# Layer 1: the 64-row update products of two neighbouring feature chunks made in one stretch

## The chip, the core and the metric

The kernel runs on one core of a Trainium2 chip. A core has TensorE (PE in the profile; its weight loads are PEld), VectorE (DVE), ScalarE (ACT), GpSimd (POOL) and SyncE (SP), which run side by side and wait for one another by semaphores. The metric is the device time of one execution, in microseconds; the figure given is the median of several executions. All arithmetic is in 32-bit floats.

## What is computed

A stack of four adaptive feed-forward layers is applied to 64 sequences of 32 tokens with 512 features, 2048 rows in all, each with a residual sum. The change lies in the second of them, called layer 1. Its first half is a gated feed-forward block in which each sequence has its own low-rank update (rank 16), chosen by an index:

```python
def lora_add(base, inp, A, B):
    Ab = A[layer_idx][lora_indices]
    Bb = B[layer_idx][lora_indices]
    t = jnp.einsum('bri,bni->bnr', Ab, inp)
    return base + jnp.einsum('bor,bnr->bno', Bb, t) * SCALE
gate = lora_add(jnp.einsum('bnh,fh->bnf', x, W_gate), x, A_gate, B_gate)
up = lora_add(jnp.einsum('bnh,fh->bnf', x, W_up), x, A_up, B_up)
act = jax.nn.silu(gate) * up
down = lora_add(jnp.einsum('bnf,hf->bnh', act, W_down), act, A_down, B_down)
```

The hidden width F is 1376. What follows (a routed mixture of low-rank experts on top of a dense product) is not touched by the change.

## The kernel before

Layer 1 takes the 2048 rows in eight groups of 256 rows, two tiles of 128 rows (t = 0 and 1). The 1376 hidden features are cut into eleven chunks f of 128 (the last, f = 10, has 96).

**Seven block products.** Gate and up of one chunk and one group are a 2 x 2 block product: the blocks of the left side are the two tiles by the two halves of the 512 input features, those of the right side are gate and up by the same halves. It is made with seven products in place of eight, `p1` to `p7` (methods of `Group`, from line 557), each of two matmuls of 128 x 128 by 128 columns, on sums of weight blocks and of activations that are made beforehand. They accumulate in three PSUM tiles, each a whole bank of 128 x 512: `acc_a`, `acc_b` and `acc_c`, each with two buffers, so that chunk f + 2 takes over the buffers of chunk f. Since later products add to the same columns, partial sums are copied out by ACT in between (`kept`, line 551): `p1` and `u2` out of `acc_a`, `p5` out of `acc_c`. The next product on those columns waits for that copy.

**The update products.** `seconds(f)` (line 586) adds the low-rank updates. The first factor, `low_x`, holds the 16 rank values of four sequences on 64 partitions, upper half for tile 0, lower half for tile 1. So each update product contracts over 64 rows only: four products for a chunk (gate and up, by tile), alternating between the upper and the lower 64 rows. Tile 0 adds to `acc_b` (gate) and `acc_c` (up), tile 1 to columns 0 to 127 (gate) and 128 to 255 (up) of `acc_a`. After them the chunk is put together: ACT copies the gate of tile 1 out of `acc_a` (line 597), DVE makes the other three blocks by adding kept partial sums (598, 599, 600), ACT takes a tanh (603), and DVE makes `actT` (604, 605), which the down projection reads later. `gate`, `up` and `sg` have one buffer each.

**The order.** TensorE's order is fixed: `on_pe` (line 76) chains every matmul to the one before. In `features(f)` it runs over two chunks: p1 of f, p7 of f - 1, p5 and p2 of f, p4 and `seconds` of f - 1, then p6 and p3 of f. So each chunk's update products stand between its p4 and the next chunk's p6. Between the chunks 0 to 4, pieces of the previous group's output are put in (`choose`, `turn`, `base`, `out`). In the first group the weight sums are made on the way (`sums_of`). The orders of the other engines are made from the program by a scheduler; waits between engines are set by it wherever two engines touch the same tile. Loads go by SP's queue (`load_by`, with an order written out), gathers of the update weights (`Bg1`, `Bu1`, `Bd1`) by POOL's.

Of the kernel before, what the change touches and what calls it, by code (L numbers as in the profile page):

```python
# [28 lines left out]
ALU = mybir.AluOpType  # L29
# [4 lines left out]
P = 128  # L34
# [7 lines left out]
FC = [(o, min(P, F1 - o)) for o in range(0, F1, P)]  # L42
# [358 lines left out]
def layer1(c, kp, x_in, x_out, sums):  # L401
# [5 lines left out]
    tc, nc, a = c.tc, c.nc, c.a  # L407
# [3 lines left out]
    NFC = len(FC)  # L411
# [5 lines left out]
    with ExitStack() as ctx:  # L417
# [31 lines left out]
        def product(out, lhsT, rhs, start, stop, more=False):  # L449
            c.on_pe(nc.tensor.matmul(out, lhsT, rhs, start=start, stop=stop, skip_group_check=more))  # L450

        class Group:
# [130 lines left out]
            def p4(self, f):  # L583
                self.block(f, 4, self.a[f])

            def seconds(self, f):

                o, w = FC[f]
                acc_a, acc_b, acc_c = (v.pop(f) for v in (self.a, self.b, self.c))
                for u in range(2):  # L590
                    for t in range(G):
                        q = slice(t * P // 2, (t + 1) * P // 2)
                        out = (acc_b, acc_c)[u][:w, :P] if t == 0 else acc_a[:w, u * P:(u + 1) * P]
                        product(out, self.B[("Bg1", "Bu1")[u]][q, o:o + w], self.low_x[q, u, :], False, True, more=True)
                part = self.part.pop(f)
                gate, up = self.gate, self.up
                nc.scalar.copy(gate[:w, 1], acc_a[:w, :P])
                nc.vector.tensor_tensor(gate[:w, 0], acc_b[:w, :P], part["p1"][:w], ALU.add)
                nc.vector.tensor_tensor(up[:w, 1], acc_a[:w, P:2 * P], up[:w, 1], ALU.add)
                nc.vector.tensor_tensor(up[:w, 0], acc_c[:w, :P], part["u2"][:w], ALU.add)  # L600
                sg = tp.tile([P, N], F32, name="sg", bufs=1)
                gate, up = (v.rearrange("p t n -> p (t n)") for v in (gate, up))
                nc.scalar.activation(sg[:w], gate[:w], AF.Tanh, scale=0.5)
                nc.vector.scalar_tensor_tensor(sg[:w], sg[:w], 1.0, gate[:w], ALU.add, ALU.mult)
                nc.vector.scalar_tensor_tensor(self.actT[:w, f, :], sg[:w], 0.5, up[:w], ALU.mult, ALU.mult)
# [92 lines left out]
        t = gup.tile([P, 3, K2, F1], F32, name="sums_gate_up")  # L698
        blocks = {1: b11, 2: b21, 3: b22, 4: b12, 5: t[:, 0], 6: t[:, 1], 7: t[:, 2]}

        def sums_of(f):

            if f >= NFC:
                return
            o, w = FC[f]
            v11, v21, v12, v22, t1, t2, t3 = (v[:, :, o:o + w] for v in
                                              (b11, b21, b12, b22, t[:, 0], t[:, 1], t[:, 2]))
            nc.vector.tensor_tensor(t1, v12, v11, ALU.subtract)
            nc.vector.tensor_tensor(t3, v22, v12, ALU.subtract)
            nc.vector.tensor_tensor(t2, v22, t1, ALU.subtract)  # L710
            nc.vector.tensor_tensor(v12, v21, t2, ALU.subtract)
# [8 lines left out]
        for g, new in enumerate(groups):  # L720
            old = groups[g - 1] if g else None
            then = groups[g + 1] if g + 1 < len(groups) else None
            parts = [f for _ in range(5) for f in next(to_sum)]

            def features(f):
                if f < NFC:
                    new.p1(f)
                if f:
                    new.p7(f - 1)
                if f < NFC:  # L730
                    new.p5(f)
                    new.p2(f)
                elif then:
                    then.x(0)
                if f:
                    new.p4(f - 1)
                    new.seconds(f - 1)
                if f < NFC:
                    new.p6(f)
                    new.p3(f)  # L740
                if g == 0:
                    sums_of(f + 2)
                if f < len(parts):
                    parts[f]()

            features(0)
            if old:
                old.choose(0)
            features(1)
            if old:  # L750
                old.choose(1)
                old.weigh(0)
            features(2)
            if old:
                old.weigh(1)
            new.load_firsts("down")
            if then:
                then.load_firsts("x")
            features(3)
            if old:  # L760
                old.turn(0)
                old.base(0)
                old.out(0)
            features(4)
            if old:
                old.turn(1)
                old.base(1)
                old.out(1)
            for f in range(AHEAD):
                new.next_down(f)  # L770
            if then:
                then.load_x()
            for f in range(5, NFC + 1):
                features(f)
            if then:
                then.load_seconds()
                then.x(1)
            new.down(range(NFC - 1), False)
            if then:
                then.x_sums()  # L780
                then.low()
            new.low_down()
            new.down((NFC - 1,), True)
# [1026 lines left out]
```

## Time and profile before

| | |
|---|---|
| three executions | 3531.25, 3531.26, 3536.69 us, median 3531.26 |
| the profiled execution's own time | 3529.51 us |
| its span, first to last instruction | 3527.7 us |
| granted TensorE clock, mean | 0.997 of full speed |
| layer 1 in it | about 380 to 1010 us |
| calls of `seconds` | 88, eight groups of eleven chunks |

The span is what the profiler saw on the core; the execution's own time has 1.8 us around it. Of the views, the timeline is used most here: every instruction with its start and length, groups of equal ones merged. A 32-bit matmul shows as two records of the same name, so a block product is four records. Starts of matmuls are measured; their ends are modelled, so that records of one engine overlap.

### The profile page before, as it was taken

What the parts mean: (1) busy time and instruction counts of PE and PEld (TensorE: products, weight loads), DVE (VectorE), ACT (ScalarE), POOL (GpSimd) and SP (SyncE); (2) the same over time, 40 slices, a digit from 0 to 9 for tenths busy, and PEclk for the clock granted to TensorE, in tenths of its full rate; (3) what the DMA queues carried; (4) which work ended last, traced back from release to release, by engine and by line L of the source; (5) the groups of instructions that cost most, each with busy time, mean ns of one, the idle gap of its engine ahead of it and who ended that gap; (6) DMA issues with size and microseconds to landing.
All of it is one profiled execution on the core that took longest, in us unless ns stands there. A gap on an engine that the chain in (4) does not pass through costs nothing.

```text
span 3527.7 us, 65667 instructions
## 1 busy us (share of the span) xinstructions
PE 3472.3 (98%) x20736; PEld 2638.2 (75%) x20736; DVE 2085.3 (59%) x5116; ACT 1537.4 (44%) x4001; POOL 1615.1 (46%) x1608
## 2 busy tenths in 40 slices
PE   8999999999999999999999999999999999999999
PEld 4444788888866778777787787877877778778755
DVE  4443533433447766766767667676676776766433
ACT  4111222222225555555555555555555555555411
POOL 0112433232336645646456455564564655645232
PEclk9999999999999999999999999999999999999999
DMA  6013554454456787878878878878878788787721
GB/s 218 24 29 129 158 162 152 151 165 145 152 186 198 251 259 245 254 248 253 257 250 259 257 247 257 257 247 263 251 253 263 249 266 257 253 256 239 238 87 59
DMA packets 630634, 735.99 MB, mean 209 GB/s; under 512 B 64274, under 2 KB 480018, under 8 KB 630290
## 3 DMA queue, kind: packets, MB, share of 16 engines
q1 hardware_dynamic: 577810, 558.74, 51.0%
q0 software_dynamic: 50176, 168.86, 13.7%
q8 instruction: 168, 2.75, 0.3%
q10 hardware_dynamic: 2304, 4.20, 0.3%
q14 instruction: 176, 1.44, 0.1%
HBM read 689.61 MB, written 41.94 MB: 207 GB/s over the span
## 4 chain that ended last, share of the span: by engine, by line
PE 90%; DVE 4%; DMA 3%; issue 1%; ACT 1%; POOL 0%; SPq 0%; DVEq 0%; ACTq 0%; POOLq 0%
PE po L913 14%; PE sc L1195 12%; PE py L913 11%; PE pq L913 9%; PE prT_ps L908 6%; PE pkv L913 5%; PE acc_a L450 5%; PE pz L450 5%; PE pd L225 4%; PE po L1575 3%; PE ph L225 3%; PE acc_c L450 3%; PE acc_b L450 2%; PE po L450 2%; PE qkT_ps L908 2%; PE py L212 2%
## 5 line engine op out<-in xcount | busy, mean ns | idle before, releaser
L939 POOL DMA_INDIRECT vt<-in_v_rows,v_rows x512 | 511.2, 998 | 305.4 <-PE po L913 186.8
L1202 ACT ACTIVATE pr<-pr,low 128x544 f32<-128x544 f32 x512 | 383.4, 749 | 545.9 <-DVE low L1200 543.9
L1195 PE MATMUL sc<-kt,qT 128*128 128x288 f32 (+1 forms) x2048 | 554.6, 393 | 9.7 <-DVE low L1200 5.7
L1195 PEld LDWEIGHTS sc<-kt,qT 128*128 128x128 f32 x2048 | 384.8, 190 | 224.3 <-issue 123.5
L913 PE MATMUL po<-prT,vt 128*128 128x128 f32 x4096 | 543.6, 276 | 3.3 <-ACT prT L1213 2.0
L913 PEld LDWEIGHTS po<-prT,vt 128*128 128x128 f32 x4096 | 522.2, 192 | 32.8 <-ACT prT L1213 13.1
L1200 DVE CUSTOM_DVE_ANT_0 pr<-sc,mask 128x544 f32<-128x544 f32 x512 | 368.2, 719 | 203.3 <-PE sc L1195 202.9
L987 POOL TENSOR_TENSOR projected<-projected,swapped 128x512 f32<-128x512 f32 x160 | 208.1, 1300 | 310.1 <-DVE projected L986 286.9
L1207 DVE TENSOR_SCALAR pr<-pr,low 128x512 f32<-128x512 f32 x512 | 317.2, 620 | 12.8
L1213 ACT COPY prT<-prT_ps 128x512 f32<-128x512 f32 x512 | 293.3, 573 | 57.7 <-PE prT_ps L908 50.6
L908 PE MATMUL prT_ps<-ident,pr 128*128 128x128 f32 x2048 | 311.3, 275 | 0.8 <-DVE pr L1207 0.7
L1204 DVE RECIPROCAL low<-low 128x1 f32<-128x1 f32 x512 | 81.9, 160 | 282.0 <-ACT pr L1202 281.8
L908 PEld LDWEIGHTS prT_ps<-ident,pr 128*128 128x128 f32 x2048 | 237.9, 142 | 8.8 <-issue 1.1
L913 PE MATMUL py<-wo,oT 128*128 128x256 f32 x1024 | 241.8, 379 | 0.0
L913 PE MATMUL pq<-wp,x_sums 128*128 128x512 f32 x512 | 240.5, 593 | 0.5 <-DVE projected L1073 0.5
L913 PEld LDWEIGHTS py<-wo,oT 128*128 128x128 f32 x1024 | 186.5, 190 | 21.1
L130 POOL TENSOR_TENSOR rs<-rs,minus_half 128x4 f32<-128x4 f32 x160 | 179.8, 1123 | 22.9 <-DVE low L1204 15.3
L913 PE MATMUL pq<-wp,xT 128*128 128x512 f32 x384 | 182.7, 599 | 5.0 <-DVE projected L1073 5.0
L913 PE MATMUL py<-wo,o_sum 128*128 128x256 f32 x768 | 181.1, 379 | 2.3 <-DVE o_sum L1131 2.1
L1205 ACT ACTIVATE own_pr<-pr,low 128x32 f32<-128x32 f32 x512 | 164.9, 322 | 41.8 <-DVE low L1204 38.9
L988 POOL TENSOR_TENSOR projected<-projected,rs 128x512 f32<-128x512 f32 x160 | 171.9, 1074 | 7.9
L946 ACT COPY own_vt<-v 32x128 f32<-32x128 f32 x512 | 150.8, 295 | 53.7 <-PE po L913 42.2
(277 smaller groups left out, 6109.2 us busy)
## 6 DMA issues: line engine op xcount, KB each, us to landing
kt<-in_kT SPq DMA_DIRECT2D x2048, 64.0 KB
wp<-in_sums SPq DMA_DIRECT2D x192, 512.0 KB
wo<-out_sums SPq DMA_DIRECT2D x128, 512.0 KB
wp<-in_WqT SPq DMA_DIRECT2D x96, 512.0 KB
wo<-in_WoT SPq DMA_DIRECT2D x96, 512.0 KB
down1T<-in_down1T SPq DMA_DIRECT2D x80, 256.0 KB
wp<-in_WkT SPq DMA_DIRECT2D x32, 512.0 KB
xt<-x SPq DMA_DIRECT2D x48, 256.0 KB
```

The costliest lines, as they stand in the source:

```text
L130: self.nc.gpsimd.tensor_tensor(t, t, self.minus_half[:, :n], ALU.pow)
L225: c.on_pe(nc.tensor.matmul(out, lhsT, rhs, start=first and i == 0, stop=last and i == len(pairs) - 1))
L450: c.on_pe(nc.tensor.matmul(out, lhsT, rhs, start=start, stop=stop, skip_group_check=more))
L908: c.on_pe(nc.tensor.transpose(pt[:, m, :], piece, c.ident))
L913: c.on_pe(nc.tensor.matmul(out, lhsT, rhs, start=first and i == 0, stop=last and i == len(pairs) - 1))
L939: nc.gpsimd.indirect_dma_start(out=vts[b % 2][:, n, :], out_offset=None, in_=a["v_rows"], in_offset=bass.IndirectOffsetOnAxis(ap=rows[h][: ...
L987: nc.gpsimd.tensor_tensor(src, src, tmp, ALU.add)
L1195: c.on_pe(nc.tensor.matmul(sc[:, lo + n * PSIZE:lo + m * PSIZE].rearrange("p (n k) -> p n k", k=PSIZE), q, kt[:, n:m, g, :], start=True, s ...
L1200: nc.vector.tensor_tensor_reduce(pr[:, :NK], sc[:, lo:lo + NK], masks[h, b], -SCALE, 3.0e38, ALU.add, ALU.min, low[:, 0:1])
L1202: nc.scalar.activation(pr[:, :NK], pr[:, :NK], AF.Exp, bias=low[:, 0:1], scale=-1.0, accum_out=low[:, 1:2])
L1207: nc.vector.tensor_scalar(pr[:, :L], pr[:, :L], low[:, 2:3], None, ALU.mult)
L1213: last_prT.append(nc.scalar.copy(prT, pt).ins)
```

## The change

`seconds(f)` is cut in two: the products stay in `seconds(f, early)`, and putting the chunk together becomes `finish(f)`. In `features(f)` with odd f, the products of f - 1 are followed at once by those of f, the chunk whose p6, p3, p7 and p4 are still to come; for even f no update products are made, and only `finish(f - 1)` follows p4. Chunk 10 has no partner and stays alone.

For an early chunk the gate product of tile 1 can't go to columns 0 to 127 of `acc_a`, since the partial sum `u2` is still to be taken from those. It goes to columns 256 to 383, ACT copies these out under the name `rest`, and in `finish` DVE adds `rest` where for other chunks ACT copies.

```diff
-            def seconds(self, f):
+            def seconds(self, f, early):
                 o, w = FC[f]
-                acc_a, acc_b, acc_c = (v.pop(f) for v in (self.a, self.b, self.c))
+                acc_a, acc_b, acc_c = (v[f] for v in (self.a, self.b, self.c))
+                at = (2 if early else 0, 1)
                 for u in range(2):
                     for t in range(G):
                         q = slice(t * P // 2, (t + 1) * P // 2)
-                        out = (acc_b, acc_c)[u][:w, :P] if t == 0 else acc_a[:w, u * P:(u + 1) * P]
+                        out = (acc_b, acc_c)[u][:w, :P] if t == 0 else acc_a[:w, at[u] * P:(at[u] + 1) * P]
                         product(out, self.B[("Bg1", "Bu1")[u]][q, o:o + w], self.low_x[q, u, :], False, True, more=True)
-                part = self.part.pop(f)
+                if early:
+                    self.kept(f, "rest", acc_a[:, 2 * P:])
+
+            def finish(self, f):
+                w = FC[f][1]
+                acc_a, acc_b, acc_c, part = (v.pop(f) for v in (self.a, self.b, self.c, self.part))
                 gate, up = self.gate, self.up
-                nc.scalar.copy(gate[:w, 1], acc_a[:w, :P])
+                if "rest" in part:
+                    nc.vector.tensor_tensor(gate[:w, 1], acc_a[:w, :P], part["rest"][:w], ALU.add)
+                else:
+                    nc.scalar.copy(gate[:w, 1], acc_a[:w, :P])
...
                 if f:
                     new.p4(f - 1)
-                    new.seconds(f - 1)
+                    if f % 2:
+                        new.seconds(f - 1, False)
+                        if f < NFC:
+                            new.seconds(f, True)
+                    new.finish(f - 1)
                 if f < NFC:
                     new.p6(f)
                     new.p3(f)
```

## The prediction

> **What bounds the kernel now.** I began with the page: engines, then the chain that ended last.
>
> ```profile
> span 3527.7 us, 65667 instructions
> PE 3472.3 (98%) x20736; PEld 2638.2 (75%) x20736; DVE 2085.3 (59%) x5116; ACT 1537.4 (44%) x4001; POOL 1615.1 (46%) x1608
> PE 90%; DVE 4%; DMA 3%; issue 1%; ACT 1%; POOL 0%; SPq 0%; DVEq 0%; ACTq 0%; POOLq 0%
> ```
>
> TensorE is the path: 98% busy, 90% of the chain. Then the stretch that the change touches, layer 1, by its window: elapsed, then PE, PEld, DVE, ACT and POOL.
>
> ```profile
> 380.00:1010.00 630.00, 626.92 (x5483) 543.14 (x5480) 243.57 (x768) 149.78 (x535) 192.73 (x237) 1.00 0.50 160
> ```
>
> PE is busy for 626.9 of 630 us at full clock; DVE (39%) and ACT (24%) are far from it. So what counts is when TensorE starts its next matmul. "Busy" hides that, because ends are modelled, so I read starts, in the timeline around one call of `seconds` (columns: start, length, engine, group).
>
> ```profile
> 496.01 0.50 PE L450 MATMUL acc_a<-xT,up1T 128*128 128x128 f32 x3
> 496.43 0.37 PE L450 MATMUL acc_b<-low_x,Bg 64*128 64x128 f32 x1
> 496.65 0.27 PE L450 MATMUL acc_b<-low_x,Bg 64*128 64x128 f32 x1
> 496.76 0.27 PE L450 MATMUL acc_c<-low_x,Bu 64*128 64x128 f32 x1
> ...
> 496.87 0.27 PE L450 MATMUL acc_c<-low_x,Bu 64*128 64x128 f32 x1
> 496.88 0.27 PE L450 MATMUL acc_a<-low_x,Bu 64*128 64x128 f32 x1
> 497.08 0.71 PE L450 MATMUL acc_a<-x_sums,sums_gate_up 128*128 128x128 f32 x4
> 497.63 0.61 PE L450 MATMUL acc_c<-x_sums,up1T 128*128 128x128 f32 x4
> ...
> 498.07 0.61 PE L450 MATMUL acc_a<-xT,gate1T 128*128 128x128 f32 x4
> ```
>
> Each f32 matmul is two records. Groups of four start 0.44 us apart (497.63, 498.07): 0.11 us a record. The eight 64-row records go in pairs, upper and lower rows side by side (each acc_b or acc_c record has an acc_a record beside it), 0.11 us a pair. The borders are what the reader is to see: last 128-row record (496.23) to first pair 0.20; first to second pair 0.22; last pair to p6 0.21; p6's own four records 0.55 instead of 0.44. Each is some 0.10 too long, together **0.39 us per stretch**, and the stretches away from the 96-wide last chunk repeat it within 0.01.
>
> **What the change removes.** Per group five odd chunks (1, 3, 5, 7, 9) move their four products into the stretch of the chunk before. Eight groups: 40 stretches of 88 go. No matmul is removed; what goes is 40 × 0.39 = **-15.5 us**, if nothing else waits. The Trainium skill (TensorEngine Tiling (Array Packing), Key Properties) has the rule behind it: changing the tiling mode drains TensorE. It gives no price; the row does.
>
> **What it adds on TensorE's path: p6 behind `rest`.** The early chunk's gate product goes to columns 256-383 of acc_a[f]; ACT copies them out as `rest`, and the very next TensorE instruction is p6(f), into columns 0-127 of the same tile. Nothing in before shows TensorE writing a bank while another engine reads other columns of it. Two answers: by addresses p6 is free to start at once; by the Trainium skill (PSUM — Partial Sum Buffer, the section on bank collisions), PSUM must be guarded by bank and quadrant, not by address. The changed program decides: in all 40 places p6's first matmul holds a wait for ACT although the p1 and p5 copies were already waited for inside the stretch; what is new on acc_a is `rest`. And on ACT `rest` stands behind the even chunk's gate copy and its tanh. These rows of before price it:
>
> ```profile
> 497.22 0.27 ACT L597 COPY gate<-acc_a 128x128 f32<-128x128 f32 x1 [1.31 <-PE acc_a L450]
> 497.52 0.42 ACT L603 ACTIVATE sg<-gate 128x256 f32<-128x256 f32 x1
> 497.84 0.25 ACT L554 COPY u<-acc_a 128x128 f32<-128x128 f32 x1
> ...
> 505.75 0.24 ACT L554 COPY u<-acc_a 96x128 f32<-96x128 f32 x1
> 506.05 0.68 PE L450 MATMUL acc_a<-x_sums,sums_gate_up 128*96 128x128 f32 x4
> ```
>
> Clock from the stretch's start (496.43). The gate copy starts at 0.79, the tanh at 1.09, and ACT's next instruction at 1.41 (497.84), 0.32 after the tanh began. In the changed stretch the last pair starts at 0.44 + 4 × 0.11 = 0.89 and ends at 1.16; ACT follows a PE end by 0.07, so `rest` is ready at 1.23, but ACT is free only at 1.41. It runs 0.25, to 1.66; TensorE follows an ACT end by 0.06 (505.99 to 506.05): p6 starts at **1.72**. Free, it would start at 0.65 + 0.44 = 1.09. The wait is 0.63 us; p6's late second record is paid either way. Per pair 0.63 - 0.39 = +0.23 (unrounded), × 40 = **+9.2 us**. By addresses it would be -15.5, by bank +9.2; I take the bank. Behind p6 on TensorE's queue stands everything else.
>
> **What is late next.**
> - p1(f+2) after an odd chunk f needs buffer acc_a[f], freed by the up add (L599). Before, it followed the stretch at once. Now the last write of acc_a[f] is p4(f): from p4's last record (0) its end is 0.275, DVE follows by 0.04, the new gate add takes 0.29, the up add 0.29, TensorE follows by 0.05: 0.95. p1's weights want to load at 0.11 × 8 = 0.89, after p6 and p3 alone. Late by 0.05, in 25 places: chunks 1, 5 and 7, and 3 in group 0 (in other groups an output tile's 4 us of matmuls lie between); 8 × 3 + 1. For chunk 1 in seven groups DVE also carries the router's small operations; p4's last record there is at 463.33, so the gate add could start at 463.64; L662, which runs 463.71 to 463.87, stands ahead of it in the changed order and takes it to 463.89, 0.25 later. That makes p1 0.30 late where it is 0.10 late now (0.71 for its group instead of 0.61):
>
> ```profile
> 464.84 0.28 DVE L599 TENSOR_TENSOR up<-acc_a,up 128x128 f32<-128x128 f32 x1
> 465.17 0.71 PE L450 MATMUL acc_a<-xT,gate1T 128*128 128x128 f32 x4
> ```
>
>   So 7 × 0.20 + 18 × 0.05 = **+2.3 us**; ends 0 and 7.5 (0.30 everywhere).
> - p7(10) waits for u2(10), as above at 506.05. Now the tanh of chunk 9 needs the new gate add, 0.60 after p4(9); tanh from 0.65, u2 at 0.97 to 1.21, p7 at 1.27. Before, p7 came 1.92 after the same record; the missing stretch is worth 0.84 (0.85 from that record to p6, less one 0.11, plus 0.10 in p6), which makes 1.08. +0.19 × 8 = **+1.5 us**; ends 0 and 1.6.
> - Group 0's first stretch holds an ACT table load of 1.28 us ahead of the tanh. It delays p7 by 1.0 now; it will delay p6 by 1.28: **+0.3 us**.
>
> **What costs nothing.** ACT loses 40 gate copies and gains 40 `rest` copies, 0.27 against 0.25. DVE gains 40 adds of 0.29, 11.6 us beside 386 idle; they count only where listed. p4(f) to p6(f+1) now follow directly, and p6 and p3 find their p1 and p5 copies done over 0.9 us earlier. p4(f) needs the up add of p7(f) (L581): from the stretch's start that ends at about 4.1, p4 would come at 4.5; cover 0.4. No DMA is issued elsewhere: SP's and POOL's orders are the same, and the loads of the next group hang on the same last stretch, chunk 10's, which stays alone. The first wait after layer 1 is DVE work behind TensorE's own products, not a DMA, so the shift is passed on whole.
>
> **Sum.** 9.2 + 2.3 + 1.5 + 0.3 = +13.3 us. The profiled execution took 3529.5 (span 3527.7): 3542.8. The median of the three runs, 3531.26, stands 1.75 above that execution, so on its footing 3544.5; I say **3544**.
>
> **Rivals.**
> - *TensorE does not stand still at p6* (faster). Evidence for: columns are disjoint; against: the wait in all 40 places. Then -15.5 + 2.3 + 1.5 = -11.7: 3519.6. The sign turns where p6's wait is under 0.39 - 3.8/40 = 0.30 us. Chance 0.05.
> - *`rest` does not queue behind the tanh*: p6 at 1.23 + 0.25 + 0.06 = 1.54, a wait of 0.45, +0.06 a pair: 2.4 + 3.8 + 0.3 = +6.5: 3537.8. Against it: the tanh stands ahead of it in ACT's order everywhere, and the gap of 0.32 was the same in each stretch I read. Chance 0.07.
> - *acc_a comes free late everywhere*: the router's pattern in all 25 places, 7.5 for 2.3: +18.5: 3549.8. For: a margin of minus 0.05 leaves no room; against: DVE is idle before most of these adds. Chance 0.13.
> - *The change doesn't merge what it says*: excluded, since the changed order has 48 stretches, 40 with eight products.
>
> The forecast keeps 0.75. Range: with the late terms at zero and the pipelining of ACT 0.03 shorter, +8: 3539; the second rival's 3538 is taken in with a margin for the runs' spread; upwards the third's 3550. 3536 to 3551 leaves out the faster case and a bit on either side. A measurement of this kernel tells 0.2% (7.1 us) from no change, about what its three runs spread. Faster 0.05; same 0.09 (half of the second rival, and a forecast with smaller terms); slower 0.86.
>
> **What would show it.** In the profile after: 48 stretches of 64-row products, forty with pairs 0.11 apart to 0.89; p6 starting some 1.72 after the stretch began, with an idle gap of about 0.56 (1.16 to 1.72) that ACT's L554 ends (40 of them, some 22 us in all); p4 of an odd chunk followed by p6 at 0.11; DVE adds onto gate from `rest`, 40 of 0.29; layer 1 longer by 12 to 14 us and the rest unchanged. Wrong if p6 starts near 1.09, or if eight products in one stretch don't keep their 0.11.

## The result, and the profile after

| | before | after |
|---|---|---|
| median of six executions each, us | 3532.64 | 3546.95 |
| lowest to highest | 3531.25 to 3538.51 | 3539.70 to 3551.78 |
| ratio, 95% interval | | 1.0034 [1.0024, 1.0045] |
| profiled execution: own time / span | 3529.51 / 3527.7 | 3539.70 / 3538.0 |
| layer 1: first 64-row product to the attention's first transpose, us | 634.46 | 645.79 |

The change makes the kernel 0.34% slower, 14.3 us between the medians. The profiled execution of the changed kernel is the fastest of its six. The page of the changed kernel:

```profile
span 3538.0 us, 65578 instructions
PE 3458.3 (98%) x20736; PEld 2627.7 (74%) x20736; DVE 2089.8 (59%) x5156; ACT 1535.4 (43%) x4001; POOL 1615.7 (46%) x1608
PE 83%; DVE 9%; issue 2%; ACT 2%; DMA 2%; SPq 1%; POOL 1%; DVEq 0%; ACTq 0%; POOLq 0%
```

The same number of matmuls, and TensorE is busy for 14 us **less** than before (3458.3 for 3472.3) in a longer span. The window of layer 1 shows where (elapsed, then PE, PEld, DVE, ACT, POOL):

```profile
380.00:1020.30 640.30, 613.25 (x5425) 535.84 (x5425) 249.01 (x812) 150.55 (x540) 192.65 (x237) 1.00 0.48 156
```

27 us of PE not busy, where before had 3 in 630. The view of waits in the same window names what it waits for (engine, tile and line <- what ended the wait: us in all, times, longest):

```profile
PEld acc_a L450 <- ACT rest L554: 31.3, 40, 2.0
...
PE acc_a L450 <- ACT rest L554: 23.6, 40, 1.8
```

Forty waits for the copy of `rest`, one for each pair of chunks. One of them in the timeline of TensorE, from p4 of an even chunk to p6:

```profile
498.77 0.37 PE L450 MATMUL acc_b<-low_x,Bg 64*128 64x128 f32 x1
...
498.99 0.27 PE L450 MATMUL acc_b<-low_x,Bg 64*128 64x128 f32 x1
...
499.10 0.27 PE L450 MATMUL acc_c<-low_x,Bu 64*128 64x128 f32 x1
...
499.65 0.27 PE L450 MATMUL acc_c<-low_x,Bu 64*128 64x128 f32 x1
499.66 0.27 PE L450 MATMUL acc_a<-low_x,Bu 64*128 64x128 f32 x1
500.48 0.71 PE L450 MATMUL acc_a<-x_sums,sums_gate_up 128*128 128x128 f32 x4 [0.55 <-ACT rest L554]
```

and ACT's timeline beside it:

```profile
499.56 0.27 ACT L607 COPY gate<-acc_a 128x128 f32<-128x128 f32 x1 [1.31 <-PE acc_a L450]
499.86 0.42 ACT L613 ACTIVATE sg<-gate 128x256 f32<-128x256 f32 x1
500.18 0.25 ACT L554 COPY rest<-acc_a 128x128 f32<-128x128 f32 x1
```

Count from the stretch's start, 498.77. The pairs keep their 0.11 us up to the last at 0.88; the matmul that `rest` copies was at 0.67, yet the copy starts at 1.41, behind the gate copy and the tanh, ends at 1.66, and p6 starts at 1.71. In all 40 stretches the median is 1.707.

### The profile page after: what moved, and what is told of

It reads as the page before. It is cut to its first block, busy times and chain, and to the rows that moved or that the text cites. A ratio compares the mean times of both kernels' runs of the same rounds, so it can differ in the third digit from the quotient of the medians.

```text
span 3538.0 us, 65578 instructions
## 1 busy us (share of the span) xinstructions
PE 3458.3 (98%) x20736; PEld 2627.7 (74%) x20736; DVE 2089.8 (59%) x5156; ACT 1535.4 (43%) x4001; POOL 1615.7 (46%) x1608
## 4 chain that ended last, share of the span: by engine, by line
PE 83%; DVE 9%; issue 2%; ACT 2%; DMA 2%; SPq 1%; POOL 1%; DVEq 0%; ACTq 0%; POOLq 0%
PE po L927 13%; PE py L927 11%; PE sc L1209 10%; PE pq L927 7%; PE prT_ps L922 5%; PE pkv L927 5%; PE pz L450 5%; PE acc_a L450 5%; PE po L1589 3%; PE pd L225 3%; PE ph L225 3%; PE acc_c L450 2%; PE po L450 2%; PE py L212 2%; PE qkT_ps L922 2%
```

## The experiments

"Layer 1" is the length defined in the table above. "Lateness" of a kind of step is summed over layer 1: how much later its records start after the ones before them than the fastest twentieth of that kind does. Ratios are against runs of before on the same chip.

**The changed kernel once more.**

> The changed kernel once more, for how much of its time is a matter of the run. From the first 64-row product of layer 1 to the first transposition of the attention (xT_ps) the kernel before took 634.5 us and the changed one 645.8 in their profiles. If the change acts in layer 1 alone, this stretch is again 645.8 within 1 us, p6 again starts 1.71 us after its stretch began, and what differs in the whole time lies outside it; ratio 1.003 to 1.004. If instead the spread of the six runs (3539.7 to 3551.8) comes from layer 1, the stretch differs by several us.

Ratio 1.0038 [1.0025, 1.0052], median 3546.80: the whole repeats. Layer 1 took 649.62, so the expectation about it missed by 3.8 us, although p6 started at 1.708 again. TensorE's waits on `acc_a` differ in one place: p4 for DVE's up add (L581). The kernel before, the first profile of the changed kernel, then this one:

```profile
PEld acc_a L450 <- DVE up L581: 4.0, 12, 0.7
...
PE acc_a L450 <- DVE up L581: 0.7, 2, 0.5
```

```profile
PEld acc_a L450 <- DVE up L581: 4.4, 14, 0.7
...
PE acc_a L450 <- DVE up L581: 1.0, 3, 0.5
```

```profile
PEld acc_a L450 <- DVE up L581: 6.2, 12, 1.1
PE acc_a L450 <- DVE up L581: 3.3, 6, 0.9
```

p4's lateness is 2.4 us more than in the first profile, most of the 3.8. So there is a second term beside `rest`, not constant from run to run, which the prediction had costed at nothing. The rest is the clock. In the first profile it was at full speed all through layer 1; here TensorE was granted half of it for 3.4 us, which costs 1.7 us (elapsed, then PE, PEld, DVE, ACT, POOL, and the granted clock behind them):

```profile
392.00:395.40 3.40, 3.40 (x19) 3.40 (x18) 0.59 (x3) 0.53 (x2) 0.76 (x1) 0.50 0.60 178
```

What set the clock back there is not shown.

**Half stretches** (before, with the gate products moved ahead of p4, so that each stretch is cut in two). It prices the entry into and exit from a stretch.

```diff
 if f:
+    new.seconds(f - 1, 0)     # gate products only
     new.p4(f - 1)
-    new.seconds(f - 1)
+    new.seconds(f - 1, 1)     # up products, then the chunk is put together
```

> The kernel before with its four 64-row products cut into two stretches, gate's ahead of p4 and up's behind it: 176 stretches in place of 88, with the same products. Theory (each stretch costs 0.39 us at its borders, whatever it holds): layer 1, from the first 64-row product to the end of its output products, longer by 88 x 0.39 = 34 us, the whole ratio about 1.0097. Rival (the 0.39 belongs to the first products after a stop of the pipeline, not to the change between 64 and 128 rows, and can hide): well under 34 us; rival (the merged stretch saved something else in e1 and e3): near 0.

Ratio 1.0088 [1.0073, 1.0104]; layer 1 666.85, +32.4 for 88 stretches more: 0.368 us a stretch, against 0.39 read off the borders. But the cut also took a wait away: in before p4 is late by 2.4 us in all behind DVE's up add, and here, with half a stretch ahead of it, by 0.1. Against the kernel before without these waits (e7 below, 631.93) it is 34.9 us, or **0.40 us a stretch**. The timeline of TensorE shows a stretch of two pairs with both its borders:

```profile
494.43 0.61 PE L450 MATMUL acc_b<-xT,gate1T 128*128 128x128 f32 x4
494.97 0.37 PE L450 MATMUL acc_b<-low_x,Bg 64*128 64x128 f32 x1
...
495.19 0.27 PE L450 MATMUL acc_b<-low_x,Bg 64*128 64x128 f32 x1
...
495.39 0.71 PE L450 MATMUL acc_a<-xT,up1T 128*128 128x128 f32 x4
496.04 0.37 PE L450 MATMUL acc_c<-low_x,Bu 64*128 64x128 f32 x1
```

Each border again adds about 0.10: 0.54 from 494.43 to 494.97 for four records that take 0.44 elsewhere (entry); 0.22 from the first pair to the second, where 0.11 is usual; 0.20 from the last pair to p4 at 495.39 (exit); and p4 takes 0.65 up to the next stretch, 0.10 for that one's entry and 0.11 for its own late second record.

**`rest` ahead of the gate copy and the tanh on ACT.** Only ACT's order is changed.

```diff
-nc.scalar.copy(gate[:w, 1], acc_a[:w, :P])
+with tc.issue_after(self.rest_copied):
+    nc.scalar.copy(gate[:w, 1], acc_a[:w, :P])
```

> As the changed kernel, but rest stands ahead of the even chunk's gate copy and tanh in ACT's order. Theory (p6 waits for the bank that rest is read from, and the tanh ahead of rest is part of the wait): rest runs from 1.23 to 1.48 us after the stretch began, p6 starts at 1.54 in place of 1.71, layer 1 is shorter than the changed kernel's by 40 x 0.17 = 7 us, about 638.8; ratio to before about 1.001 to 1.002. Rival (what ACT does ahead of rest doesn't matter, p6 waits for something else): p6 stays at 1.71 and the time at the changed kernel's.

Ratio 1.0018 [1.0009, 1.0027]; layer 1 639.61; p6 at 1.527. ACT's timeline, then TensorE's p6:

```profile
500.19 0.27 ACT L554 COPY rest<-acc_a 128x128 f32<-128x128 f32 x1 [1.73 <-PE acc_a L450]
500.36 0.27 ACT L609 COPY gate<-acc_a 128x128 f32<-128x128 f32 x1
500.66 0.42 ACT L617 ACTIVATE sg<-gate 128x256 f32<-128x256 f32 x1
```

```profile
499.88 0.27 PE L450 MATMUL acc_a<-low_x,Bu 64*128 64x128 f32 x1
500.51 0.71 PE L450 MATMUL acc_a<-x_sums,sums_gate_up 128*128 128x128 f32 x4 [0.36 <-ACT rest L554]
```

`rest` now starts 0.04 after the last product's end (499.88 + 0.27), and p6 still stands still for 0.36. So of the wait of some 0.62, ACT's queue makes 0.18 (1.707 - 1.527) and the copy's own way, PE to ACT to PE, the rest of it. It also shows that the copy waits for the *last* product into acc_a, not for its own.

**The early products in banks that p6 does not write.** The gate of tile 0 goes to acc_a's second quarter, tile 1 to acc_b's second and third; `rest` is copied out of acc_b. DVE gets one add more in 40 chunks.

```diff
-out = (acc_b, acc_c)[u] if t == 0 else acc_a[:, at[u] * P:...]
+if early:
+    out = (acc_c[:, :P] if u else acc_a[:, P:2 * P]) if t == 0 else acc_b[:, (1 + u) * P:(2 + u) * P]
...
-    self.kept(f, "rest", acc_a[:, 2 * P:])
+    self.kept(f, "rest", acc_b[:, P:2 * P])
...
+nc.vector.tensor_tensor(gate[:w, 0], acc_a[:w, P:2 * P], gate[:w, 0], ALU.add)   # in finish
```

> The early chunk's tile-1 products go to acc_b and its gate product of tile 0 to columns 128 to 255 of acc_a, so that rest is copied out of acc_b and p6 follows the stretch without waiting for ACT. One DVE add more for each of the 40 early chunks. Theory (the merged stretch saves 0.39 us a pair and the wait of p6 for rest costs 0.61): p6 starts 1.09 us after the stretch began, layer 1 from the first 64-row product to the attention's first transposition takes 634.5 - 15.5 + about 2 = 621 us, the whole 0.9960 to 0.9970 of before. Rival (eight products in one stretch save nothing, or the chunk's putting together at the end is what costs): p6 at 1.09 but the stretch 634 us or more, ratio 1.000 or above.

Ratio 0.9978 [0.9968, 0.9987]. TensorE's timeline at the end of a stretch that starts at 498.04:

```profile
498.92 0.27 PE L450 MATMUL acc_c<-low_x,Bu 64*128 64x128 f32 x1
498.93 0.27 PE L450 MATMUL acc_b<-low_x,Bu 64*128 64x128 f32 x1
499.13 0.71 PE L450 MATMUL acc_a<-x_sums,sums_gate_up 128*128 128x128 f32 x4
```

p6 at 1.09 with no gap: the whole wait came from p6 writing the bank that the copy reads, not from the eight products in a row. But layer 1 took 627.4, not the 621 expected. The view of waits has the rest:

```profile
PEld acc_a L450 <- DVE up L581: 12.8, 20, 1.2
...
PE acc_a L450 <- DVE up L581: 8.5, 18, 1.0
```

The second term again. At the 128-wide chunks p4 is late by 8.2 us in all, three times as much as in the changed kernel (2.9). Chunk 10's p4 comes on top: it is held alike in every group, so that the lateness does not show it, and starts 0.47 us later than in before, 3.7 us in all. The two groups kept apart (count, busy time, mean length, then the idle time before them and what ended it):

```profile
L450 PE MATMUL acc_a<-xT,up1T 128*128 128x128 f32 x320 | 50.6, 281 | 4.1 <-DVE up L581 4.0
L450 PE MATMUL acc_a<-xT,up1T 128*96 128x128 f32 x32 | 5.4, 292 | 4.5 <-DVE up L581 4.5
```

DVE has an add more here; whether that is why p4 waits longer is looked into in the last experiment.

**The early products ahead of p4.** As in the changed kernel, but with both `seconds` calls before `p4(f - 1)`, so that p4's 0.44 us cover the copy.

```diff
 if f:
+    if f % 2:
+        new.seconds(f - 1, False)
+        if f < NFC:
+            new.seconds(f, True)
     new.p4(f - 1)
-    if f % 2:
-        ...
     new.finish(f - 1)
```

> As the changed kernel, bank and rest included, but the merged stretch stands ahead of p4 of the even chunk in place of behind it, so that p4's 0.45 us lie between the stretch and p6, and the gate copy and tanh come behind rest on ACT. Theory: rest is done at 1.48, p6 would come at 1.64 anyway, so its wait is gone: the gain of 15.5 us shows, less 26 p1 that wait about 0.09 us more for acc_a (the gate copy now follows p4): layer 1 about 622 to 624 us, ratio 0.9963 to 0.9975. Rival (reading a bank while TensorE goes on in others costs by itself, or merging saves nothing): 634 or more.

Ratio 0.9988 [0.9979, 0.9997]; layer 1 629.15, 5 us over what was expected. The lateness of p6 is gone (26.5 to 0), but p4's second record is now late by 4.9 in all (1.0 in the changed kernel), and the transposes of the next group wait for ACT (weight load, then matmul):

```profile
PEld xT_ps L486 <- ACT xT L487: 6.2, 7, 0.9
...
PE xT_ps L486 <- ACT xT L487: 4.7, 7, 0.7
```

These were not taken apart further.

**p7's sum taken out by ACT.** If p4 waits because L581 stands in DVE's queue, it should not wait when ACT, which is idle there, copies p7's columns out (as `p7`), and DVE adds `p5` to the copy later, in `finish`. Tried on all three: the kernel with other banks (e5), the changed kernel (e6), before (e7).

```diff
-nc.vector.tensor_tensor(self.up[:w, 1], self.a[f][:w, :P], self.part[f]["p5"][:w], ALU.add)   # p7
+self.kept(f, "p7", self.a[f])
...
-nc.vector.tensor_tensor(up[:w, 1], acc_a[:w, P:2 * P], up[:w, 1], ALU.add)                    # finish
+nc.vector.tensor_tensor(part["p7"][:w], part["p7"][:w], part["p5"][:w], ALU.add)
+nc.vector.tensor_tensor(up[:w, 1], acc_a[:w, P:2 * P], part["p7"][:w], ALU.add)
```

> As e1_other_banks, and ACT copies acc_a after p7 (128x128) in place of DVE's up add, so that p4 waits for ACT and no longer for what stands in DVE's queue; DVE adds p5 to the copy later. Theory (e1 lost some 10 us of its gain in p4's waits for that DVE add, behind DVE instructions which GpSimd's adds stretch from 0.42 to 0.83 us): p4's waits of 10 to 12 us go, layer 1 at 615 to 618 us against 627.4, ratio to before about 0.995. Rival (DVE, with 128 instructions more, or ACT, with 88 more, becomes what is late): layer 1 at 627 or above.

> The changed kernel with the same ACT copy after p7, bank and wait of rest as in the changed kernel. Theory (the two profiles of the changed kernel differ by 3.8 us in layer 1 through p4's waits for DVE, which depend on when GpSimd's adds fall): p4's waits go, layer 1 at 642 to 644 us, the wait of p6 for rest unchanged at 1.71 after the stretch's start, ratio about 1.0025. Rival (the spread comes from elsewhere): layer 1 between 645 and 650.

> The kernel before with the same ACT copy after p7 alone, to tell what of e5 is merging. Theory: only p4's own waits of before, some 2.3 us, go: layer 1 at 632 us, ratio 0.9985 to 1.0000; so e5 less this one is what merging is worth, 15 us. Rival (the copy by ACT is most of e5's gain): near e5.

| | ratio to before, 95% | layer 1, us | p6 after the stretch's start |
|---|---|---|---|
| e5, other banks | **0.9943 [0.9930, 0.9957]** | 614.74 | 1.092 |
| e6, changed kernel | 1.0021 [1.0012, 1.0030] | 644.70 | 1.708 |
| e7, before | 0.9993 [0.9984, 1.0002] | 631.93 | 0.645 |

In all three p4 is late by 0.2 us or less in all. In e5 the waits of TensorE's weight loads on `acc_a` come down to:

```profile
PEld acc_a L450 <- ACT p L554: 1.5, 7, 0.6
...
PEld acc_a L450 <- ACT u L554: 0.6, 1, 0.6
```

e5 against e7 is the merging with no wait at p6: 17.2 us, or 0.43 a pair; 1.3 us of it is p1, which is less late in e5 (0.7 us in all, 1.9 in e7), and without that it is 0.40. e5 against e6 is the same merged kernel with the wait at p6: 30.0 us, of which 1.7 are a stretch at half the clock in e6's layer 1, as in the repeat. And e5 is faster than both before and the changed kernel: 3511.83 against 3531.40 of before on its chip. e6's eleven runs still spread over 11 us (3534.18 to 3545.17), so the spread of whole times is not p4's waits alone. Here it goes with the clock: the four executions with a mean granted clock of 0.998 took 3534.18 to 3536.26, the four with 0.996 took 3537.92 to 3545.17. That is not all of it, for five of the changed kernel's first six runs, all at 0.997, spread from 3539.70 to 3550.35. What makes up the rest stays open.

**GpSimd's subtractions left out.** Why was DVE late at all? In the eleven profiles with the subtractions, 26 to 32 of the 176 last products of a chunk (`sg` and `actT`) took over 0.55 us, most of them 0.83, instead of 0.42. This is the kernel with other banks, with GpSimd's four subtractions left out that make the attention's weight sums, so that its attention computes something else. The kernel with other banks was run once more beside it on the same chip, one execution each.

```diff
-nc.gpsimd.tensor_tensor(t1, b12, b11, ALU.subtract)
-nc.gpsimd.tensor_tensor(t3, b22, b12, ALU.subtract)
-nc.gpsimd.tensor_tensor(t2, b22, t1, ALU.subtract)
-nc.gpsimd.tensor_tensor(t4, b21, t2, ALU.subtract)
-c.last_sum = nc.gpsimd.dma_start(dst, t).ins
+c.last_sum = nc.gpsimd.dma_start(dst, w[0]).ins
```

> The early products in banks that are not written next (as e1_other_banks), and GpSimd's four subtractions that make the weight sums of the attention left out (the blocks are written in their place, so the attention's result is not the reference's). In e1_other_banks layer 1 took 627.4 us, some 6 more than its merged stretches alone explain, and TensorE's p4 waited for DVE's up add (L581) 12.8 us as weight load and 8.5 us as matmul, while 28 of DVE's 176 last products of a chunk (over 0.55 us, median 0.83 against 0.42) all overlapped one of these subtractions. Theory (these subtractions slow DVE, and the slow DVE instructions are what makes p4 wait): the slow instructions go from 28 to under 3, p4's weight-load wait for L581 falls to under 5 us, and layer 1 takes 618 to 622 us. Rival (DVE's queue in front of L581 is too long for p4's cover even at 0.42 us): few slow instructions as well, but p4's wait stays above 9 us and layer 1 at 625 to 629.

> The kernel of e1_other_banks once more, on the same chip as e8_no_adds, to know how far its layer 1 (627.4 us) and p4's waits for L581 (12.8 us as weight load) repeat. Every theory: layer 1 within 4 us of 627.4, since the changed kernel's own differed by 3.8 between two profiles; 25 to 32 slow DVE instructions.

Without the subtractions: 1 instruction over 0.55 us (27 in the second run with them), layer 1 619.98 against 626.04, the whole 3515.32 against 3523.01, p4's first record in the 128-wide chunks late by 0.05 us in all against 5.02. The theory's length holds; its "under 5" for the weight-load wait does not quite:

```profile
PEld acc_a L444 <- DVE up L575: 6.4, 8, 1.2
```

These eight (L575 is L581 there, the lines having moved by six) are p4 of chunk 10, once in each group. TensorE's row of one of them shows the gap:

```profile
422.28 0.68 PE L444 MATMUL acc_a<-xT,up1T 128*96 128x128 f32 x4 [0.51 <-DVE up L575]
```

DVE's instructions ahead of it there have their short lengths (0.43, 0.42, 0.28), so in this place the rival is right: the queue itself is too long. The idle time ahead of chunk 10's p4 is 4.5 us in all, as it was with the subtractions, while that of the other chunks went from 4.1 to 0.0. So in the kernel with other banks p4's waits at the 128-wide chunks come from the subtractions, and the 3.7 us at chunk 10 do not. The likely cause there is the add that DVE does more; it was not tested alone.

## Why the prediction was right, and where not

Forecast 3544, measured 3546.95, within 3536 to 3551; as a difference, +13.3 was worked out and the medians differ by 14.3. Layer 1 was to be longer by 12 to 14 us: it was +11.3 in the first profile and +15.2 in the repeat, 1.7 of that the clock. The terms, with what layer 1 of the first profile shows (+11.3 in all):

| step | predicted | measured |
|---|---|---|
| p6 behind `rest`, less the stretch saved, per pair | +0.23 | +1.062 - 0.738 - 0.102 = +0.222 |
| the same, 40 pairs | +9.2 | +8.9 |
| group 0's table load | +0.3 | +0.28 |
| p7(10) behind u2 | +1.5 | +1.28 (8 × 0.160) |
| p1(f + 2) behind the up add of an odd chunk | +2.3 | none |
| p4 behind L581 | 0 | +0.4; about +2.9 in the repeat |
| p6 of the last group's first pair, at 2.25 in place of 1.71 | - | +0.5 |

(1.062 is how much later p6 starts after its stretch's start than before, 1.707 - 0.645; 0.738 the odd chunk's own stretch that no longer lies between p4 and p6; 0.102 the p6 record that is no longer late.)

**The main step was right**, in mechanism and size: p6 at 1.71 where 1.72 was worked out. Both halves of it were tested apart: with nothing read from acc_a it starts at 1.09, as the sum had it for "free", and with `rest` ahead of the tanh at 1.527, where the second rival said 1.54. The price of a stretch, 0.39, is 0.40 by the half stretches and 0.40 by e5 against e7, each with the other waits taken out. That p6 must wait for a copy of *other columns of its bank* was taken from the program's waits and from the Trainium skill's rule (PSUM — Partial Sum Buffer, the section on bank collisions), by which PSUM is guarded by bank and quadrant. The wait is one that the program holds. What the chip would do without it no run shows, since no kernel was tried whose p6 ran into the bank during the copy; e1 shows only that a different bank takes the wait away.

**Two terms failed, and hid one another.** One was 2.3 us too large, the other 0.4 to 2.9 too small, so that the sum came nearer than its parts: that much of the hit is luck. The lateness of p1(f + 2), +2.3, was oversized: it took the two adds on DVE one behind the other at 0.29 each. In the changed kernel's timeline of DVE the second starts 0.21 after the first:

```profile
495.75 0.29 DVE L605 TENSOR_TENSOR gate<-acc_a,rest 128x128 f32<-128x128 f32 x1 [1.05 <-PE acc_a L450]
495.96 0.28 DVE L609 TENSOR_TENSOR up<-acc_a,up 128x128 f32<-128x128 f32 x1
```

so that acc_a is free at 496.24, not at 496.33, and p1 at 496.44 has no gap before it. A lateness of 0.05 lay within what the term left out: adjacent instructions overlap. The larger part of the term, 7 × 0.20 at chunk 1, failed for the same reason: the gate add begins 0.08 after the router's small operation ahead of it, before that has ended, and the up add 0.20 after the gate add. So acc_a is free at 463.02 in the first of these places, and p1 follows on time at 463.09. For ACT the sum did use starts (0.32 after the tanh began); for DVE it used lengths.

"p4 needs the up add of p7: cover 0.4, costs nothing" was the other. Before's own waits, shown with the repeat above, had p4 held by that add already (4.0 us as weight load, 2.7 of them at chunk 10). The cover is there when DVE's instructions have their short length; beside GpSimd's subtractions many have about twice that, and then the 0.4 is gone. The chain in DVE's timeline, in the kernel with other banks:

```profile
488.10 0.42 DVE L618 SCALAR_TENSOR_TENSOR sg<-sg,gate 128x256 f32<-128x256 f32 x1 [0.57 <-ACT sg L617]
488.55 0.83 DVE L619 SCALAR_TENSOR_TENSOR actT<-sg,up 128x256 f32<-128x256 f32 x1
489.49 0.29 DVE L581 TENSOR_TENSOR up<-acc_a,p 128x128 f32<-128x128 f32 x1
```

and TensorE's p4 at its end:

```profile
489.84 0.71 PE L450 MATMUL acc_a<-xT,up1T 128*128 128x128 f32 x4 [0.16 <-DVE up L581]
```

In before's own rows there were 30 such instructions; the prediction had read only the short ones. With L581 on ACT the waits go (e5, e6, e7), with the subtractions gone all but chunk 10's go (e8).

**The rivals.** That p6 does not stand still fell with the first profile. That `rest` is not behind the tanh is what the chip does only when told so. That acc_a is late everywhere came as near to the median with its 3549.8, but its mechanism did not appear: p1's lateness is no larger than before (0.8 us in all, 1.1 before).

## What to carry to other kernels

Merging small products saves a fixed price per stretch, but look at the bank that the next matmul writes: where a copy made necessary by the merge still reads it, and the program makes the matmul wait, the saving of about 0.40 a pair became a loss of 0.22, and placing the side products in other banks turned it back. Price a cover of a few tenths of a microsecond with the longest form of what is queued in it, not with the typical one, and take the time between starts, not the lengths, where instructions of one engine follow one another. Where the engine on the path waits for a busy one, hand its release to an idle one: a copy by ACT, with DVE's add put off until later, cost 88 more instructions and took p4's waits from 2.4 us to 0.2 in the kernel before. By itself that gained nothing clear of noise there (0.9993 [0.9984, 1.0002]); with other banks, where these waits were longer, layer 1 became 11.3 us shorter on the same chip (626.04 to 614.74).

## What the chip showed that was not expected

**A DVE instruction that reads two SBUF operands waits until a running GpSimd subtraction has ended.** DVE's timeline and GpSimd's in the changed kernel:

```profile
492.15 0.43 DVE L614 SCALAR_TENSOR_TENSOR sg<-sg,gate 128x256 f32<-128x256 f32 x1 [0.16 <-ACT sg L613]
492.61 0.84 DVE L615 SCALAR_TENSOR_TENSOR actT<-sg,up 128x256 f32<-128x256 f32 x1
493.37 0.28 DVE L608 TENSOR_TENSOR gate<-acc_b,p 128x128 f32<-128x128 f32 x1
```

```profile
492.30 0.86 POOL L366 TENSOR_TENSOR sums<-blocks 128x256 f32<-128x256 f32 x1 [2.67 <-DMA in_sums<-sums]
493.12 0.91 POOL L367 TENSOR_TENSOR sums<-blocks 128x256 f32<-128x256 f32 x1
```

The instruction at 492.61 begins while the subtraction of 492.30 runs until 493.16, and ends 0.29 after it. Another pair from the same profile, with less of the subtraction left:

```profile
872.18 0.56 DVE L614 SCALAR_TENSOR_TENSOR sg<-sg,gate 128x256 f32<-128x256 f32 x1 [0.16 <-ACT sg L613]
```

```profile
871.73 0.72 POOL L368 TENSOR_TENSOR sums<-blocks,sums 128x256 f32<-128x256 f32 x1
```

The subtraction ends at 872.45, the DVE instruction again 0.29 later. All 30 instructions of this profile that took over 0.55 us begin during such a subtraction. Of the full-width ones (128 x 256), 33 begin with more than 0.15 us of a subtraction left, between 0.17 and 0.66, and every one ends 0.28 to 0.29 us after it; with less left they keep their 0.42. So they are not slowed by a factor: twice the length, 0.83, is only the commonest case. If the two had gone on side by side at half speed, an instruction with 0.66 left would have taken some 0.75 us (0.42 + 0.66 / 2, an estimate from these lengths); it took 0.94. The other order shows the same: 25 subtractions begin while such a DVE instruction has more than 0.15 us left, and each ends 0.58 to 0.59 us after that, where 0.72 is its length alone. In e8, with no subtractions, one long instruction is left, and it ends 0.29 us after another GpSimd operation, the addition onto `xt`. The adds out of PSUM are not touched: 51 of them lie wholly inside a subtraction, and their median is 0.291 us, as of all others.

This agrees with the Trainium skill (SBUF — State Buffer, the section on its two separate sides), by which VectorE with two SBUF inputs and a GpSimd instruction that reads SBUF take a shared port pair in turn, as a lock: the one that starts first holds it, and the other is blocked. GpSimd's spans in the profile are rough, but an end that follows within 0.01 us in all 33 places leaves little room for sharing.

**Sixteen 64-row records in a row keep 0.11 us a pair.** Nothing in before showed more than eight.
